# Layer norm of two graph layers: from ScalarE with relu to VectorE without, relu in the copy after the transpose

## The chip, the cores and the metric

The kernel runs on one core of a Trainium2 chip. The core has five engines that run side by side, each with its own queue of instructions in a fixed order: TensorE (PE, with its weight loads PEld), VectorE (DVE), ScalarE (ACT), GpSimd (POOL) and SyncE (SP). [...] The metric is the device time of one execution in microseconds (us), as the median of several runs; 0.2% of it is about 10 us.

## The reference

64 graphs of 256 nodes with 128 features each, and one 256 x 256 matrix `adj` for all. Four layers follow each other; each takes a layer norm without learned scale, a relu, and a graph layer, and adds the result:

```
h = maximum(layernorm(x), 0);  x = x + layer0(h)   # attention over all pairs of nodes
h = maximum(layernorm(x), 0);  x = x + layer1(h)   # elu(h Wi), sigmoid gates, two products
h = maximum(layernorm(x), 0);  x = x + layer2(h)   # tanh-limited attention
h = maximum(layernorm(x), 0);  x = x + layer3(h)   # five gated steps
layernorm(x) = (x - mean) / sqrt(var + 1e-5)       # over the 128 features
```

Layer 0 is the costly one. For each pair (i, j) of nodes it needs sum over e of a[e] * leaky_relu(s1[i, e] + s2[j, e]) with 256 values of e, so 64 x 256 x 256 x 256 elements pass an elementwise engine before TensorE sums them. Layers 1, 2 and 3 are small products.

## The kernel before, in words

The 64 graphs go in 34 groups: 1, 1, thirty times 2, 1, 1. A group's node features lie as `[128 nodes, G, 128 features]`, with G = 4 blocks of 128 nodes in a group of two graphs and G = 2 in a group of one.

Pair work of layer 0 (class `Pairs`). A tile is 128 x 256 elements. ScalarE (L620) makes a tile with relu and a bias column, GpSimd (L625) with min and max, VectorE (L608) makes four at a time as a "half". Four of the 128 x 512 slices that TensorE multiplies (L673) form a batch; there are two batches for each of 32 rows of a graph, one for each half of e. Where five batches or more are ready for TensorE as a row begins, the row is "merged": only the first half of e is made as a tile, VectorE adds the second to it in place (L642, "merge"), and TensorE has one batch less to multiply. VectorE's and ScalarE's operand s2 is held in PSUM (`s_dve`, `s_act`), GpSimd's in SBUF. The tiles `r` have 10 buffers.

Everything else is written as generators that yield the name of the engine of their next step: `head` and `senders` (layer 0 ahead of the pairs), `softmax0` (behind them), `first_rest` (layers 1 and 2, and the norm of layer 3) and `last_rest` (layer 3). They stand in four chains. The loop at the end of the kernel is a planner: it keeps a clock for each engine, books a cost for each instruction (the helpers `dve`, `act`, `pool` and `mm`, and the costs in `Model`), and at each turn issues what can start first by its clocks. A chain has a due time for each step, so that its steps spread over the pair work. The order of the instructions on each engine is thus fixed when the kernel is built, and follows from the booked costs. A changed cost changes which engine gets the next tile, and which rows are merged.

The norm is `ln_relu`. VectorE takes the statistics (L418, L421). GpSimd forms ve = var + eps (L426), minus = -mean (L427), rstd = ve to the power -0.5 (L429) and shift = minus * rstd (L431), all with G columns. ScalarE forms h = relu(rstd * x + shift), one 128 x 128 block an instruction (L437), with two operands that are columns of one value per node. The G blocks are issued two by two. `transpose_blocks` then transposes h on TensorE into PSUM, and ScalarE copies it to SBUF (L452) for the whole group. Layers 1 and 2 use h for nothing but this transpose. Layers 0 and 3 also use h itself.

In layers 1 and 2 together there are 256 blocks in 68 norms (34 groups, two layers).

Of the kernel before, what the change touches and what calls it, by code (L numbers as in the profile page):

```python
# [8 lines left out]
F32 = mybir.dt.float32  # L9
AF = mybir.ActivationFunctionType  # L10
ALU = mybir.AluOpType

P = 128
# [13 lines left out]
def flat(t):  # L27
    return t.rearrange("p a b -> p (a b)")


def sizes(xt):

    blocks = xt.shape[1]
    return blocks, blocks // 2, blocks * P
# [19 lines left out]
def kernel(ctx: ExitStack, tc: tile.TileContext, ins: dict, out: bass.AP):  # L54
# [8 lines left out]
    bp = ctx.enter_context(tc.tile_pool(name="act", bufs=1))  # L63
    sp = ctx.enter_context(tc.tile_pool(name="small", bufs=3))
# [11 lines left out]
    def psum_a(shape, name):  # L76
        return ps_a.tile(shape, F32, tag="ps_a", name=name)
# [8 lines left out]
    def dve(n, pointers=0, more=0):  # L86
        model.op("dve", 66 + n * 1.042 + 60 * pointers + more)
        return nc.vector

    def act(n, pointers=0, sbuf=0, table=0, more=0):  # L90
        model.op("act", 40 + n * 0.833 + 42 * sbuf + (0, 103, 196)[pointers] + 49 * table + more)
        return nc.scalar

    def pool(ns):
        model.op("pool", ns)
        return nc.gpsimd

    def mm(out, lhsT, rhs, **flags):


        n = 1
        for d in rhs.shape[1:]:
            n *= d
        model.op("pe", max(n, 64) * 1.676)
        for c in range(4):
            nc.tensor.matmul(  # L106
                out[bass.ts(c, 32), :], lhsT=lhsT[:, bass.ts(c, 32)], rhs=rhs, **flags
            )

    def tr(out, src):  # L110
        mm(out, lhsT=src, rhs=ident, start=True, stop=True)
# [294 lines left out]

    def ln_relu(space, xt, tag, ln, when=None):

        G = xt.shape[1]
        for g in range(G):
            if g % 2 == 0:
                yield "dve", when
            if g == 0:
                st = sp.tile([P, G, 6], F32, tag=tag + "_st", name="bst", bufs=2)
                mv = sp.tile([P, G, 2], F32, tag=tag + "_mv", name="bmv", bufs=2)
            dve(P).bn_stats(st[:, g, :], xt[:, g, :])  # L418
        yield "dve"
        for g in range(G):  # L420
            dve(6, more=15).bn_aggr(mv[:, g, :], st[:, g, :])  # L421
        yield "pool"

        ve = sp.tile([P, G], F32, tag=tag + "_ve", name="bve", bufs=2)
        minus = sp.tile([P, G], F32, tag=tag + "_mm", name="bmm", bufs=2)
        pool(277).tensor_scalar(ve, mv[:, :, 1], 1.0, LN_EPS, ALU.mult, ALU.add)  # L426
        pool(150).tensor_scalar(minus, mv[:, :, 0], -1.0, 0.0, ALU.mult, ALU.add)  # L427
        rstd = sp.tile([P, G], F32, tag=tag + "_rs", name="brs", bufs=2)
        pool(1085).tensor_tensor(rstd, ve, neg_half[:, 0:G], ALU.pow)  # L429
        shift = sp.tile([P, G], F32, tag=tag + "_sh", name="bsh", bufs=2)  # L430
        pool(302).tensor_tensor(shift, minus, rstd, ALU.mult)  # L431
        for g in range(G):
            if g % 2 == 0:
                yield "act"
            if g == 0:
                h = space.tile([P, G, P], F32, tag=ln, name=tag, bufs=3 if space is ap else 1)
            act(P, 2, 1).activation(  # L437
                h[:, g, :], xt[:, g, :], AF.Relu, bias=shift[:, g : g + 1],
                scale=rstd[:, g : g + 1],
            )  # L440
        return h

    def transpose_blocks(space, src, tag, banks):

        yield "pe"
        G, _, W = sizes(src)
        tp = banks([P, G, P], tag + "_ps")
        for g in range(G):
            tr(tp[:, g, :], src[:, g, :])
        yield "act"  # L450
        t = space.tile([P, G, P], F32, tag=tag, name=tag)
        act(W).copy(t, tp)  # L452
        return t


# [295 lines left out]

    def layer1(x1):
        G, NB, W = sizes(x1)
        h = yield from ln_relu(bp, x1, "h1", "h")
        h_t = yield from transpose_blocks(bp, h, "h_t", psum_a)
        yield "pe"
        xh_ps = psum_a([P, W], "xh_ps")
        mm(xh_ps, lhsT=wi, rhs=flat(h_t), start=True, stop=True)
        xh_t = yield from elu(xh_ps, bi, "xh_t", "xh_t")

        for b in range(NB):
            yield "pe"
            y_ps = psum_a([P, 2, P + 1], "y1_ps")
            for c in range(2):
                mm(
                    y_ps[:, c, :], lhsT=xh_t[:, bass.ts(2 * b + c, P)], rhs=wn1,
                    start=True, stop=True,
                )
            yield "act"
            if b == 0:  # L770
                y = bp.tile([P, G, P], F32, tag="y1", name="y1")
                a_src = sp.tile([P, G], F32, tag="a_src", name="a_src")
            act(N).copy(y[:, bass.ts(b, 2), :], y_ps[:, :, 0:P])
            yield "dve"
            dve(2, 1).tensor_scalar(
                a_src[:, bass.ts(b, 2)], y_ps[:, :, P], 0.5, be_h, ALU.mult, ALU.add
            )
        yield "pe"
        tgt_ps = psum_a([P, W], "tgt_ps")
        mm(tgt_ps, lhsT=wt_rep, rhs=xh_t, start=True, stop=True)  # L780
        yield "pool"
        x1b = bp.tile([P, G, P], F32, tag="x1b", name="x1b")
        counts["x1"] += 1
        pool(1265).tensor_tensor(
            x1b, x1, bm_bc.unsqueeze(1).to_broadcast([P, G, P]), ALU.add
        )

        ths, e_ts = [], []
        for b in range(NB):
            yield "act"  # L790
            th = bp.tile([P, 2, N], F32, tag="th", name="th", bufs=2)
            for jc in range(2):
                act(N, 1).activation(
                    th[:, jc, :], tgt_ps[:, bass.ts(b, N)], AF.Tanh,
                    bias=a_src[:, 2 * b + jc : 2 * b + jc + 1], scale=0.5,
                )
            ths.append(th)
        for b in range(NB):
            yield "dve"
            e_t = bp.tile([P, 2, N], F32, tag="e_t", name="e_t", bufs=2)  # L800
            dve(2 * N, more=200).scalar_tensor_tensor(e_t, ths[b], 1.0, mask_h, ALU.add, ALU.mult)
            e_ts.append(e_t)
        yield "pe"
        rsum_ps = psum_a([P, W], "rsum_ps")
        for b in range(NB):
            for jc in range(2):
                mm(
                    rsum_ps[:, bass.ts(b, N)], lhsT=ones, rhs=e_ts[b][:, jc, :],
                    start=(jc == 0), stop=(jc == 1),
                )  # L810
        yield "dve"
        self_t = bp.tile([P, W], F32, tag="elu_m", name="self_t")
        dve(W).tensor_tensor(self_t, rsum_ps, xh_t, ALU.mult)
        yield "pe"
        rc_ps = psum_a([P, W], "rc_ps")
        for b in range(NB):
            for jc in range(2):
                mm(
                    rc_ps[:, bass.ts(b, N)], lhsT=y[:, b * 2 + jc, :], rhs=e_ts[b][:, jc, :],
                    start=(b == 0 and jc == 0), stop=False, skip_group_check=True,  # L820
                )
        mm(rc_ps, lhsT=wn2, rhs=self_t, start=False, stop=True, skip_group_check=True)
        rc_t = yield from elu(rc_ps, bn, "rc_t", "h")
        yield "pe"
        o1_ps = psum_a([P, G, P], "o1_ps")
        for g in range(G):
            mm(
                o1_ps[:, g, :], lhsT=rc_t[:, bass.ts(g, P)], rhs=wm[:, 0, :], start=True, stop=False
            )
            mm(  # L830
                o1_ps[:, g, :], lhsT=xh_t[:, bass.ts(g, P)], rhs=wm[:, 1, :], start=False, stop=True
            )
        yield "dve"
        x2 = bp.tile([P, G, P], F32, tag="x2", name="x2")
        dve(W).tensor_tensor(x2, o1_ps, x1b, ALU.add)
        return x2

    def layer2(x2, when):
        G, NB, W = sizes(x2)
        h = yield from ln_relu(bp, x2, "h2", "h")  # L840
        h_t = yield from transpose_blocks(bp, h, "h_t", psum_a)
        yield "pe"
        g_ps = psum_a([P, W], "g_ps")
        mm(g_ps, lhsT=qk, rhs=flat(h_t), start=True, stop=True)
# [202 lines left out]
    while True:  # L1047
        paced = n < len(graphs) - 2
        if not making and n < len(graphs) and "s2" in sent[n]:
            g, b = graphs[n]  # L1050
# [96 lines left out]
```

## Time and profile before

| what | us |
|---|---|
| median of 3 runs | 5171.33 (5164.48 to 5172.37) |
| profiled execution | 5160.42 |
| its span | 5158.4 |
| TensorE busy | 5066.5 |
| ScalarE busy | 5032.3 |
| VectorE busy | 4983.9 |
| GpSimd busy | 4895.8 |

The profile is of one execution. It gives each instruction's start and end, the engine, the line of the kernel and the tiles it writes and reads. In a row of groups the columns are line, engine, operation, written tile <- read tiles, shapes and count, then the busy time in us and the mean duration of one in ns, and then the time that the engine stood idle just before such instructions, with what ended it. Rows of the stages give the stretch, its length, the busy time of the five engines with counts, the granted TensorE clock and the DMA share. A row of waits gives who waited for whom, the sum in us, how often, and the longest. A duration is not always what an instruction costs: on ScalarE several records overlap, so that the step from one instruction to the next is shorter than the duration of either.

### The profile page before, as it was taken

Reading aid. Unit: us, or ns where it says so; the run is one execution under the profiler, and the core shown is the slowest. Engines: PE = TensorE matmul, PEld = TensorE weight load, DVE = VectorE, ACT = ScalarE, POOL = GpSimd, SP = SyncE. Lnnn points to the kernel's source line nnn. Section 1 sums busy time; section 2 is a strip of 40 time slices with the busy share of each in tenths; the row PEclk is TensorE's granted clock in tenths of the full one; section 3 lists DMA queues with packets and bytes.
Section 4 is the critical chain, followed back from the end, with each engine's and each line's share of the span. In section 5 each row is a group of like instructions: output and inputs, shape, how many; then the busy total and the mean of one; then the engine's idle time right before and its main releaser. Section 6 shows DMA issues by size and latency. Waiting matters only on the chain. (4 is left out here: it accounts for less than half of the span.)

```text
span 5158.4 us, 172489 instructions
## 1 busy us (share of the span) xinstructions
PE 5066.5 (98%) x66800; PEld 2359.4 (46%) x66800; DVE 4983.9 (97%) x9900; ACT 5032.3 (98%) x13224; POOL 4895.8 (95%) x10829
## 2 busy tenths in 40 slices
PE   8999999999999999999999999999999999999996
PEld 4545444436444444544444544544444444444443
DVE  7999999999999999999999999999999999999993
ACT  7999999999999999999999999999999999999993
POOL 8999999999999999999999999999999999999991
PEclk9999999999999999999999999999999999999999
DMA  0000000000000000000000000000000000000000
GB/s 21 6 2 5 5 6 6 6 2 6 6 6 6 2 6 6 6 6 6 2 6 6 6 6 2 6 6 6 6 3 5 6 6 5 5 2 4 6 4 6
DMA packets 56104, 29.33 MB, mean 6 GB/s; under 512 B 20336, under 2 KB 55280, under 8 KB 55280
## 3 DMA queue, kind: packets, MB, share of 16 engines
q1 hardware_dynamic: 53168, 17.97, 1.4%
q8 instruction: 523, 8.57, 0.7%
q14 instruction: 301, 2.47, 0.2%
q10 hardware_dynamic: 2112, 0.33, 0.0%
HBM read 9.84 MB, written 8.45 MB: 4 GB/s over the span
## 5 line engine op out<-in xcount | busy, mean ns | idle before, releaser
L625 POOL TENSOR_SCALAR r<-s,s1n 128x256 f32<-128x256 f32 x10204 | 4646.6, 478 | 101.6 <-PE e_ps L673 33.9
L620 ACT ACTIVATE r<-s_act,s 128x256 f32<-128x256 f32 x9976 | 4593.3, 1478 | 10.5 <-PE e_ps L673 10.4
L673 PE MATMUL e_ps<-r,a_win 128*32 128x512 f32 x27632 | 3380.6, 593 | 8.3 <-DVE r L642 2.8
L642 DVE SCALAR_TENSOR_TENSOR r<-s_dve,s1n,r 128x256 f32<-128x256 f32 x5136 | 2094.4, 472 | 2.5 <-ACT r L620 1.5
L608 DVE TENSOR_TENSOR r<-s_dve,s1n 128x1024 f32<-128x1024 f32 x1735 | 2017.6, 1211 | 7.3 <-PE e_ps L673 1.4
L673 PEld LDWEIGHTS e_ps<-r,a_win 128*32 128x32 f32 x27632 | 1098.4, 110 | 1590.4 <-issue 1124.7
L620 ACT ACTIVATE r<-s,s 128x256 f32<-128x256 f32 x512 | 381.2, 1667 | 0.0
L437 ACT ACTIVATE h<-x,bsh,brs 128x128 f32<-128x128 f32 x384 | 329.5, 1384 | 3.6 <-POOL bsh L431 2.3
L929 ACT ACTIVATE gate_ps<-gate_ps,bz 128x512 f32<-128x512 f32 (+1 forms) x170 | 269.6, 1586 | 7.6 <-PE gate_ps L106 7.6
L910 ACT COPY m_t<-m_ps 128x512 f32<-128x512 f32 (+1 forms) x170 | 260.9, 1535 | 13.9 <-PE m_ps L106 13.9
L931 ACT ACTIVATE hv_ps<-hv_ps,bh 128x512 f32<-128x512 f32 (+1 forms) x170 | 266.4, 1567 | 7.6 <-PE hv_ps L106 7.6
L106 PE MATMUL m_ps<-adj_t,hn 128*32 128x256 f32 x4096 | 269.0, 381 | 3.7 <-ACT hn L452 3.6
L916 ACT ACTIVATE m_ps<-gate_ps,br 128x512 f32<-128x512 f32 (+1 forms) x170 | 256.8, 1511 | 10.9 <-PE gate_ps L106 10.7
L452 ACT COPY hn<-hn_ps 128x512 f32<-128x512 f32 (+1 forms) x136 | 208.1, 1530 | 24.1 <-PE hn_ps L106 24.0
L106 PEld LDWEIGHTS m_ps<-adj_t,hn 128*32 128x32 f32 x4096 | 157.4, 110 | 113.2 <-issue 32.3
L697 ACT ACTIVATE pm<-e_ps,nmax 128x256 f32<-128x256 f32 x128 | 194.5, 1526 | 2.2 <-DVE nmax L688 2.2
L106 PE MATMUL gate_ps<-m_t,t_w_w 128*32 128x512 f32 (+1 forms) x1360 | 187.9, 574 | 8.7 <-ACT m_t L910 7.7
L106 PE MATMUL gate_ps<-m_t,w_t 128*32 128x512 f32 (+1 forms) x1360 | 185.2, 568 | 4.9 <-ACT m_ps L916 4.9
L106 PE MATMUL hv_ps<-m_t,t_w_w 128*32 128x512 f32 (+1 forms) x1360 | 185.1, 568 | 0.0
L106 PE MATMUL hv_ps<-rh,u_th 128*32 128x512 f32 (+1 forms) x1360 | 184.9, 567 | 0.0
L106 PE MATMUL hn_ps<-ident,hf 128*32 128x128 f32 x4096 | 162.8, 274 | 19.8 <-DVE hf L941 19.8
L106 PEld LDWEIGHTS hn_ps<-ident,hf 128*32 128x32 f32 x4096 | 136.4, 110 | 84.5 <-issue 62.5
(206 smaller groups left out, 5952.2 us busy)
## 6 DMA issues: line engine op xcount, KB each, us to landing
xt<-in_x_dram SPq DMA_DIRECT2D x30, 256.0 KB
out_dram<-y SPq DMA_DIRECT2D x30, 256.0 KB
row<-rows SPq DMA_DIRECT2D x128, 0.5 KB
xt<-in_x_dram SPq DMA_DIRECT2D x4, 128.0 KB
out_dram<-y SPq DMA_DIRECT2D x4, 128.0 KB
bound<-row SPq DMA_DIRECT2D x30, 2.0 KB
raw_L_gnn_w_w<-in_L_gnn_w_w_dram SPq DMA_DIRECT2D x3, 128.0 KB
adj_n<-in_adj_dram ACTq DMA_DIRECT2D x1, 256.0 KB
```

The source lines that it names most:

```text
L106: nc.tensor.matmul(out[bass.ts(c, 32), :], lhsT=lhsT[:, bass.ts(c, 32)], rhs=rhs, **flags)
L437: act(P, 2, 1).activation(h[:, g, :], xt[:, g, :], AF.Relu, bias=shift[:, g : g + 1], scale=rstd[:, g : g + 1],)
L452: act(W).copy(t, tp)
L608: nc.vector.tensor_tensor(r[:, 2 * g2 : 2 * g2 + 2, :, :], s2[:, ec : ec + 1, :].unsqueeze(1).to_broadcast([P, 2, 2, N]), self.s1n_v[:, ec ...
L620: nc.scalar.activation(r[:, g, ic, :], s2[:, ec, :], AF.Relu, bias=s1[:, ec, i : i + 1])
L625: nc.gpsimd.tensor_scalar(r[:, g, ic, :], s2[:, ec, :], FLT_MAX, s1n[:, ec, i : i + 1], ALU.min, ALU.max,)
L642: nc.vector.scalar_tensor_tensor(r[:, g, ic, :], self.own("dve")[:, 1, :], self.of["s1n"][:, 1, i : i + 1], r[:, g, ic, :], ALU.max, ALU.add,)
L673: nc.tensor.matmul(self.e_ps[bass.ts(g, 32), :, :].rearrange("p a b -> p (a b)"), lhsT=a_win[:, batch["ec"], 31 - t : 63 - t], rhs=flat(r[ ...
L910: act(W).copy(m_t, m_ps)
L916: act(W, 1).activation(t_r, g_ps, AF.Tanh, bias=br, scale=0.5)
L929: act(W, 1).activation(t_z, g_ps, AF.Tanh, bias=bz, scale=0.5)
L931: act(W, 1).activation(cand, hv_ps, AF.Tanh, bias=bh)
```

## The change

For layers 1 and 2, `ln_relu` no longer forms minus and shift on GpSimd, and ScalarE no longer forms h. VectorE forms (x - mean) * rstd instead, block by block, from SBUF to SBUF, with the mean and rstd columns as operands. The relu, which now is missing there, is taken after the transpose: the copy from PSUM to SBUF becomes an activation with relu. Relu works element by element, so that its place before or after the transpose makes no difference to h. Layers 0 and 3 stay as they were. The planner books the new costs, and so plans the whole program anew.

```diff
-    def ln_relu(space, xt, tag, ln, when=None):
+    def ln_relu(space, xt, tag, ln, when=None, relu=True):
...
         ve = sp.tile([P, G], F32, tag=tag + "_ve", name="bve", bufs=2)
-        minus = sp.tile([P, G], F32, tag=tag + "_mm", name="bmm", bufs=2)
         pool(277).tensor_scalar(ve, mv[:, :, 1], 1.0, LN_EPS, ALU.mult, ALU.add)
-        pool(150).tensor_scalar(minus, mv[:, :, 0], -1.0, 0.0, ALU.mult, ALU.add)
+        if relu:
+            minus = sp.tile([P, G], F32, tag=tag + "_mm", name="bmm", bufs=2)
+            pool(151).tensor_scalar(minus, mv[:, :, 0], -1.0, 0.0, ALU.mult, ALU.add)
         rstd = sp.tile([P, G], F32, tag=tag + "_rs", name="brs", bufs=2)
         pool(1085).tensor_tensor(rstd, ve, neg_half[:, 0:G], ALU.pow)
-        shift = sp.tile([P, G], F32, tag=tag + "_sh", name="bsh", bufs=2)
-        pool(302).tensor_tensor(shift, minus, rstd, ALU.mult)
+        if relu:
+            shift = sp.tile([P, G], F32, tag=tag + "_sh", name="bsh", bufs=2)
+            pool(302).tensor_tensor(shift, minus, rstd, ALU.mult)
         for g in range(G):
             if g % 2 == 0:
-                yield "act"
+                yield "act" if relu else "dve"
             if g == 0:
                 h = space.tile([P, G, P], F32, tag=ln, name=tag, bufs=3 if space is ap else 1)
-            act(P, 2, 1).activation(
-                h[:, g, :], xt[:, g, :], AF.Relu, bias=shift[:, g : g + 1],
-                scale=rstd[:, g : g + 1],
-            )
+            if relu:
+                act(P, 2, 1).activation(
+                    h[:, g, :], xt[:, g, :], AF.Relu, bias=shift[:, g : g + 1],
+                    scale=rstd[:, g : g + 1],
+                )
+            else:
+                dve(P // 2, 1, more=20).tensor_scalar(
+                    h[:, g, :], xt[:, g, :], mv[:, g, 0:1], rstd[:, g : g + 1],
+                    ALU.subtract, ALU.mult,
+                )
         return h

-    def transpose_blocks(space, src, tag, banks):
+    def transpose_blocks(space, src, tag, banks, relu=False):
...
         t = space.tile([P, G, P], F32, tag=tag, name=tag)
-        act(W).copy(t, tp)
+        if relu:
+            act(W, table=1).activation(t, tp, AF.Relu)
+        else:
+            act(W).copy(t, tp)
         return t
...
     def layer1(x1):
-        h = yield from ln_relu(bp, x1, "h1", "h")
-        h_t = yield from transpose_blocks(bp, h, "h_t", psum_a)
+        h = yield from ln_relu(bp, x1, "h1", "h", relu=False)
+        h_t = yield from transpose_blocks(bp, h, "h_t", psum_a, relu=True)
...
     def layer2(x2, when):
-        h = yield from ln_relu(bp, x2, "h2", "h")
-        h_t = yield from transpose_blocks(bp, h, "h_t", psum_a)
+        h = yield from ln_relu(bp, x2, "h2", "h", relu=False)
+        h_t = yield from transpose_blocks(bp, h, "h_t", psum_a, relu=True)
```

## The prediction

> **What bounds the kernel now.** I read the page first: busy shares, the chain that ended last, the costliest groups.
>
> ```profile
> PE 5066.5 (98%) x66800; PEld 2359.4 (46%) x66800; DVE 4983.9 (97%) x9900; ACT 5032.3 (98%) x13224; POOL 4895.8 (95%) x10829
> ...
> PE 12%; ACT 9%; DVE 2%; issue 1%; POOL 0%; ACTq 0%; POOLq 0%; DVEq 0%
> ...
> L625 POOL TENSOR_SCALAR r<-s,s1n 128x256 f32<-128x256 f32 x10204 | 4646.6, 478 | 101.6 <-PE e_ps L673 33.9
> L620 ACT ACTIVATE r<-s_act,s 128x256 f32<-128x256 f32 x9976 | 4593.3, 1478 | 10.5 <-PE e_ps L673 10.4
> ...
> L642 DVE SCALAR_TENSOR_TENSOR r<-s_dve,s1n,r 128x256 f32<-128x256 f32 x5136 | 2094.4, 472 | 2.5 <-ACT r L620 1.5
> L608 DVE TENSOR_TENSOR r<-s_dve,s1n 128x1024 f32<-128x1024 f32 x1735 | 2017.6, 1211 | 7.3 <-PE e_ps L673 1.4
> ...
> L437 ACT ACTIVATE h<-x,bsh,brs 128x128 f32<-128x128 f32 x384 | 329.5, 1384 | 3.6 <-POOL bsh L431 2.3
> ```
>
> No engine is idle, so shares don't name the bound. Then the split by stage (start, pair phase, tail), and ScalarE's waits in the pair phase:
>
> ```profile
> 0.00:60.00 60.00, 44.76 (x480) 17.77 (x484) 33.05 (x89) 27.75 (x70) 39.17 (x97) 0.91 0.15 38
> 60.00:5039.00 4979.00, 4943.12 (x65012) 2304.46 (x65008) 4915.54 (x9728) 4966.61 (x13068) 4851.58 (x10718) 1.00 0.02 5
> 5039.00:5158.40 119.40, 78.57 (x1320) 37.16 (x1312) 35.27 (x85) 37.98 (x89) 5.08 (x16) 0.96 0.02 6
> ...
> ACT r L620 <- PE e_ps L673: 6.4, 7, 2.6
> ACT m_ps L916 <- PE gate_ps L106: 2.7, 3, 1.1
> ACT h L437 <- POOL bsh L431: 1.4, 3, 0.7
> ```
>
> The columns are PE, weight loads, DVE, ACT, POOL. In 4979 us ScalarE waits about 12 us in all. A record of ScalarE overlaps its neighbours (mean 1478 ns), so I take costs from the records as the step from one end to the next: ScalarE tile 364 ns (mean 366), norm block L437 381, copy of a 128x512 block 476, GpSimd tile 454, VectorE half (L608, four tiles) 1132, merge (L642) 392. Cost times count leaves of the 4979 us: ScalarE 16 us of waiting beside 31 us of spread, VectorE 79, GpSimd 138. TensorE at 858 ns for a batch of eight passes, 54 and 27 ns for narrower passes, is left with 134. ScalarE is the late engine. The planner books 357 ns for its tile where the trace has 364 to 366, so it runs behind its plan, while VectorE and GpSimd keep theirs and wait. The chain agrees: 9% ScalarE against 2% VectorE.
>
> [...] The one table load in the trace is the first; I expect no other.
>
> Evidence on the new operation[...], from the timeline (start, length of the row, count; the last row is GpSimd beside the row above it):
>
> ```profile
> 7.28 1.11 DVE L264 TENSOR_SCALAR perm<-places,place,a_abs 128x128 f32<-128x128 f32 x4
> ...
> 165.15 0.68 DVE L801 SCALAR_TENSOR_TENSOR e_t<-th,mask_h 128x512 f32<-128x512 f32 x1
> ...
> 74.31 1.57 DVE L392 TENSOR_TENSOR raw_L_gnn_w_w<-raw_L_gnn_w_w 128x128 f32<-128x128 f32 x1
> ...
> 1314.76 2.85 DVE L801 SCALAR_TENSOR_TENSOR e_t<-th,mask_h 128x512 f32<-128x512 f32 x1
> ...
> 1314.60 3.27 POOL L625 TENSOR_SCALAR r<-s,s1n 128x256 f32<-128x256 f32 x6
> ```
>
> L264 has the new form exactly (128x128, SBUF to SBUF, two column operands) with GpSimd idle: one takes 342 ns, so the step is (1110-342)/3 = 256 ns. L801 and L392 have two SBUF inputs with GpSimd busy. L801 takes 0.68 us free, but its 64 run from 673 to 2854 ns, median 733; the 2854 ns one let four GpSimd tiles pass and then cost the fifth some 530 ns. By where in the GpSimd tile they start: from 0 to about 100 ns none waits, from 110 to 330 they wait until about 335 or 450, later ones rarely.
>
> **The change part by part.** Counts are those of the built program.
>
> - ScalarE loses 256 norm blocks: 256 x 0.381 = -97.5 us. 68 copies become relu (+12 ns each, taking the 488 ns of L866, an activation without columns): +0.8. The planner hands it 200 more tiles: 200 x 0.366 = +73.2. Sum **-23.5 us**.
> - GpSimd loses 68 times minus (151 ns) and shift (304 ns; 298 for two columns): -30.9. 28 more tiles at 454: +12.7. Sum **-18.2**. [...]between 0 (L364 and L367, [...]cost the GpSimd tile beside them nothing) and 150 ns each (beside L392); I take 30, +8 us, hidden in its 138 us of waits. At 150 it is +38, still hidden.
> - TensorE has 3 batches fewer: **-2.6**. It is no bound.
> - VectorE gains 256 operations of cost c, loses 63 halves (-71.3), gains 24 merges (+9.4).
>
> What c is decides. The planner books 66 + 64 x 1.042 + 60 + 20 = 213 ns. Lower bound 256, L264's. [...]for a block at a random place in the GpSimd tile, about 80 ns, and 25 for an occasional lost turn (one L801 of 64, one L392 of 3). The blocks stand in pairs: the second asks 256 ns after the first was let in, inside the next GpSimd tile's hold after a first that waited, so it waits some 195, otherwise some 90; mean 140. So c = 256 + (105 + 140)/2 = **378 ns**; the upper end I keep is 600 (lost turns common). VectorE then has 4900 - 71.3 + 9.4 + 96.8 = **4935 us**; ScalarE 4932 - 23.5 + 31 spread = **4940**. The block also brings VectorE a new wait, for rstd from GpSimd. ScalarE's wait on GpSimd at L437 was 1.4 us in the pair phase, so I cost it at nothing; were the power late, merges and halves would stand behind the block on VectorE's queue, TensorE's next batch would wait for those, and r buffers would come free later. [...]
>
> Two engines now stand level where one stood at the top with 16 us of waits. I add 30 us, between ScalarE's 16 and VectorE's 79: 4935 + 30 = 4965, that is **-14 us** for the pair phase.
>
> The start has no block of these layers. In the tail layer 3 of the last groups sets the end: the norms of the last group lie beside it, so their saving is worth nothing. But in the built order the last pair batch is followed by one 256-wide m_ps product and one gate product less (5047.4 to 5050.0 in the trace before): **-2.5**. GpSimd is idle there[...].
>
> Sum -16 on the profiled 5160.4 us (span 5158.4): about 5145. The runs' median, 5171.3, is 11 us higher, so I shift by the same: 5171 - 16 = **5155 us**.
>
> **Rivals.**
>
> - *Little contention; ScalarE stays the bound.* If c is at most 339 (where 4838 + 256 c + 30 reaches 4979 - 23.5 = 4955.5), the pair phase falls by ScalarE's 23.5 us: with the tail -26, **5145**. For: L364 and L367 ran beside busy GpSimd tiles with next to no delay. [...] Against: the L801 rows.
> - *A draw.* c near 450: each block of a pair is let in once per GpSimd tile. VectorE 4953 + 30 = 4983, +4 - 2.5: **5173**.
> - *Slower[...].* The place is the block pairs; the price is a lost turn of 451 ns or more. From c = 443 the time is no better than before, from 483 it is over 0.2% slower; at 600 VectorE has 4992 + 30 = 5022, +43 - 2.5: **5212**. For: the 1.57 and 2.85 us rows, two of 67. Against: the median L801 waits only 60 ns[...].
> - That the change doesn't do what it says: the built program shows the moved instructions, and the other blocks keep their counts. No chance given.
>
> **How the numbers follow.** Forecast 48%, ScalarE-bound 20%, draw 12%, starvation 20%. A measurement tells some 0.2% (10 us) from no change. Of the forecast, 40 points are faster and 8 within it (c up to 420 or so). Faster 0.40 + 0.20 = 0.60; same 0.08 + 0.12 = 0.20; slower 0.20. Range 5140 to 5186: below the second case by the spread of the runs, up through the draw and the beginning of starvation, leaving out its worse half and the luckiest few. The likeliest case's own range is 5147 to 5165.
>
> **What would show it.** The block on VectorE: a step near 378 ns, minimum durations near 342, many 150 to 250 longer, a few over 1 us. ScalarE's waits in the pair phase up from 12 us; VectorE's down from 79; GpSimd tiles beside a block longer than 474 ns. Still one table load. Pair phase ending near 5025. I am wrong on c if the block's median is near 342 (second case) or its mean above 600 (fourth); wrong on the bound if VectorE still waits 80 us and the time hasn't moved.

## The result and the profile after

The changed kernel takes **5224.07 us** (median of 5 runs, 5216.57 to 5231.55). The kernel before takes 5172.37 beside it (5 runs, 5164.48 to 5175.45). The ratio is 1.0099, with an interval of 1.0087 to 1.011: about 52 us slower, where 16 us faster was forecast. The profiled execution took 5216.57 us, its span is 5214.7.

The page of the kernel after: busy times, the chain that ended last, and the costliest groups.

```profile
PE 5083.4 (97%) x66776; PEld 2396.5 (46%) x66776; DVE 5088.6 (98%) x10117; ACT 5024.6 (96%) x13168; POOL 4909.7 (94%) x10721
...
PE 1%; ACT 1%; DVE 1%; issue 0%; ACTq 0%; DVEq 0%
...
L637 POOL TENSOR_SCALAR r<-s,s1n 128x256 f32<-128x256 f32 x10232 | 4686.8, 522 | 131.9 <-PE e_ps L685 62.8
L632 ACT ACTIVATE r<-s_act,s 128x256 f32<-128x256 f32 x10176 | 4445.1, 1195 | 21.7 <-PE e_ps L685 21.1
...
L654 DVE SCALAR_TENSOR_TENSOR r<-s_dve,s1n,r 128x256 f32<-128x256 f32 x5160 | 2105.6, 469 | 0.6 <-POOL r L637 0.4
L620 DVE TENSOR_TENSOR r<-s_dve,s1n 128x1024 f32<-128x1024 f32 x1672 | 1944.0, 1208 | 7.1 <-PE tgt_ps L106 0.5
```

VectorE's busy time is up by 105 us, ScalarE's and GpSimd's hardly move. The counts are the planned ones. The chain is followed back only a short way here and tells nothing. By stage (stretch, then busy time of PE, weight loads, DVE, ACT, POOL):

```profile
0.00:60.00 60.00, 44.59 (x476) 17.66 (x480) 33.03 (x89) 27.67 (x70) 39.28 (x97) 0.91 0.15 38
60.00:5095.00 5035.00, 4959.96 (x65011) 2341.52 (x65004) 5014.17 (x9927) 4960.80 (x13017) 4866.61 (x10615) 1.00 0.02 5
5095.00:5214.70 119.70, 78.80 (x1304) 37.32 (x1296) 41.43 (x104) 36.10 (x83) 3.80 (x10) 0.95 0.02 6
```

The whole loss lies in the pair phase: the weights of the last pair product are loaded at 5105.3 us, before at 5046.6, and from there to the end it is 109.4 us against 111.8. In that phase ScalarE now waits for VectorE; in the kernel before its largest wait was 6.4 us:

```profile
ACT rc_ps L757 <- DVE elu_m L755: 22.4, 24, 2.1
ACT r L632 <- PE e_ps L685: 17.1, 16, 4.5
ACT pm L709 <- DVE nmax L700: 13.9, 14, 1.8
```

In the same phase VectorE's own longest wait in sum is 1.1 us; in the kernel before (second row) it was 9.4:

```profile
DVE elu_m L755 <- PE rc_ps L106: 1.1, 2, 0.6
...
DVE rc_t L749 <- ACT elu_m L746: 9.4, 14, 1.3
```

VectorE is the bound. What fills it beyond the plan is not the new blocks (L446). It is an instruction that the change doesn't touch, e_t in layer 1: L813 here, L801 before. These are the rows of groups after (busy us, then mean ns of one):

```profile
L813 DVE SCALAR_TENSOR_TENSOR e_t<-th,mask_h 128x512 f32<-128x512 f32 x64 | 133.4, 2084 | 0.0
...
L446 DVE TENSOR_SCALAR h<-x,bmv,brs 128x128 f32<-128x128 f32 x256 | 106.9, 457 | 2.6 <-POOL brs L431 2.5
```

and this is the same row of the kernel before:

```profile
L801 DVE SCALAR_TENSOR_TENSOR e_t<-th,mask_h 128x512 f32<-128x512 f32 x64 | 51.7, 808 | 0.0
```

Those 64 instructions cost VectorE 82 us more. The timeline after, at the longest of them (start, length, count; then who waited):

```profile
4817.00 9.66 POOL L637 TENSOR_SCALAR r<-s,s1n 128x256 f32<-128x256 f32 x20
4818.90 6.96 DVE L813 SCALAR_TENSOR_TENSOR e_t<-th,mask_h 128x512 f32<-128x512 f32 x1
...
4825.91 1.93 PE L106 MATMUL rsum_ps<-e_t,ones 128*32 128x256 f32 x16 [3.77 <-DVE e_t L813]
```

The e_t at 4827.31 us, with no GpSimd tile beside it, takes 0.68 us. The one at 4818.90 takes 6.3 us more, and fourteen GpSimd tiles start in its time, some 453 ns apart. Each tile that starts during such a wait is a lost turn below. VectorE starts nothing else until 4825.78, and TensorE waits 3.77 us. No list of waits has this wait, and e_t's idle time before it is 0.0. It shows only as a long record. 30 of the 64 take over 1.1 us; in the profile before it was one.

One more difference counts below. The mean record of a GpSimd tile is 522 ns here and was 478 before, although the step from tile to tile stays at 451 to 454 ns. Within a row of tiles without a pause the records grow by about 1.3 ns a tile, so that each comes to overlap the next by 100 to 150 ns in place of 20 to 30. I call such executions "growing" and the others "quiet". In the runs from here on a trace shows the first of several executions, and its kind need not be that of the others. In one run below, e12, the first took some 80 us less than the others, so that its ratio means nothing; I use medians there.

### The profile page after: what moved, and what is told of

Read it like the earlier page. It is cut to its first block, busy times and chain, and to the rows that moved or that the text cites. A ratio compares the mean times of both kernels' runs of the same rounds, so it can differ in the third digit from the quotient of the medians.

```text
span 5214.7 us, 172615 instructions
## 1 busy us (share of the span) xinstructions
PE 5083.4 (97%) x66776; PEld 2396.5 (46%) x66776; DVE 5088.6 (98%) x10117; ACT 5024.6 (96%) x13168; POOL 4909.7 (94%) x10721
## 5 line engine op out<-in xcount | busy, mean ns | idle before, releaser
L632 ACT ACTIVATE r<-s_act,s 128x256 f32<-128x256 f32 x10176 | 4445.1, 1195 | 21.7 <-PE e_ps L685 21.1
L685 PE MATMUL e_ps<-r,a_win 128*32 128x512 f32 x27608 | 3427.5, 593 | 18.3 <-DVE r L654 14.0
L620 DVE TENSOR_TENSOR r<-s_dve,s1n 128x1024 f32<-128x1024 f32 x1672 | 1944.0, 1208 | 7.1 <-PE tgt_ps L106 0.5
L922 ACT COPY m_t<-m_ps 128x512 f32<-128x512 f32 (+1 forms) x170 | 207.3, 1219 | 26.0 <-PE m_ps L106 26.0
L941 ACT ACTIVATE gate_ps<-gate_ps,bz 128x512 f32<-128x512 f32 (+1 forms) x170 | 220.6, 1298 | 6.8 <-PE gate_ps L106 6.6
L928 ACT ACTIVATE m_ps<-gate_ps,br 128x512 f32<-128x512 f32 (+1 forms) x170 | 210.9, 1241 | 16.0 <-PE gate_ps L106 12.3
L943 ACT ACTIVATE hv_ps<-hv_ps,bh 128x512 f32<-128x512 f32 (+1 forms) x170 | 219.1, 1289 | 7.3 <-PE hv_ps L106 7.3
L106 PE MATMUL gate_ps<-hf,u_t 128*32 128x512 f32 (+1 forms) x1088 | 164.7, 573 | 0.0
L106 PE MATMUL s_ps<-h0t,w_p 128*32 128x256 f32 (+1 forms) x1568 | 160.4, 449 | 4.1 <-ACT s1n L487 2.5
```

What stands on the lines that cost most here:

```text
L106: nc.tensor.matmul(out[bass.ts(c, 32), :], lhsT=lhsT[:, bass.ts(c, 32)], rhs=rhs, **flags)
L620: nc.vector.tensor_tensor(r[:, 2 * g2 : 2 * g2 + 2, :, :], s2[:, ec : ec + 1, :].unsqueeze(1).to_broadcast([P, 2, 2, N]), self.s1n_v[:, ec ...
L632: nc.scalar.activation(r[:, g, ic, :], s2[:, ec, :], AF.Relu, bias=s1[:, ec, i : i + 1])
L685: nc.tensor.matmul(self.e_ps[bass.ts(g, 32), :, :].rearrange("p a b -> p (a b)"), lhsT=a_win[:, batch["ec"], 31 - t : 63 - t], rhs=flat(r[ ...
L922: act(W).copy(m_t, m_ps)
L928: act(W, 1).activation(t_r, g_ps, AF.Tanh, bias=br, scale=0.5)
```

## The experiments

Theory 1: e_t's lost turns are the whole loss. Theory 2: the loss is the plan's (new order, the blocks as such), and the long e_t only shows it. Theories A, B and C then ask why e_t loses more turns after the change: A, the blocks of layer 1 ahead of it disturb GpSimd; B, the whole plan has shifted; C, GpSimd lacks the small operations minus and shift. (In the expectations of e1 and e2, A and B still stand for another question: whether the tiles grow by the program or by the chip.)

### Both kernels again (e1, e2), and e_t with an operand in PSUM (e3, e4)

e1 and e2 are the kernels as they are. e3 (before) and e4 (after) share this edit, here shortened. It leaves out the mask, so the values of e_t are others; the instruction, its size and its place stay:

```diff
-            dve(2 * N, more=200).scalar_tensor_tensor(e_t, ths[b], 1.0, mask_h, ALU.add, ALU.mult)
+            w = tgt_ps.rearrange("p (c n) -> p c n", n=N) if NB == 2 else ...   # the target product, in PSUM
+            dve(2 * N, more=200).scalar_tensor_tensor(e_t, ths[b], 1.0, w, ALU.add, ALU.mult)
```

> The kernel before, unchanged, profiled once more on the chip of the next runs. In the profile of the changed kernel GpSimd's tiles last 522 ns on the mean (478 before) because each ends a little later after its start than the one in front of it (about +1.3 ns a tile), and e_t lasts 2084 ns (808 before). Theory A, the changed program does this: here tiles stay near 474 to 478 ns and e_t near 0.8 us. Theory B, it is the chip or the day of the profile: here tiles creep too, and e_t exceeds 1.5 us.

> The changed kernel, unchanged, profiled on the same chip. Theory A: tiles near 520 ns, e_t near 2 us, time near 5224. Theory B: the same values as the kernel before has on this chip.

> The kernel before, with e_t = (th + 1) * (target product in PSUM) in place of the mask in SBUF: the mask is left out, the instruction, its size and its place are the same, but it has one SBUF input[...]. All theories: e_t falls from 0.81 to 0.68 us, 64 x 0.13 = 8 us of VectorE, which waits 79 us anyway: 5160 to 5172.

> The changed kernel with the same edit. Theory 1, the loss is e_t's lost turns[...] (64 x 1.28 us = 82 us more on VectorE): 5150 to 5165, that is 5 to 20 us under the kernel before with the same edit. Theory 2, the 256 blocks themselves overload VectorE (391 ns each) and the new order adds waits: the time stays 30 us or more over the kernel before with the same edit, 5200 or more.

On this chip before takes 5176.29 us (15 runs). e1 took 5174.08 and e2 5233.38, one execution each. The rows of e_t and of GpSimd's tile in e1:

```profile
L801 DVE SCALAR_TENSOR_TENSOR e_t<-th,mask_h 128x512 f32<-128x512 f32 x64 | 75.5, 1180 | 0.0
...
L625 POOL TENSOR_SCALAR r<-s,s1n 128x256 f32<-128x256 f32 x10204 | 4662.9, 530 | 100.4 <-PE e_ps L673 33.2 <-ACT s L514 16.5 <-ACT e_ps L726 13.0
```

and in e2:

```profile
L813 DVE SCALAR_TENSOR_TENSOR e_t<-th,mask_h 128x512 f32<-128x512 f32 x64 | 146.5, 2289 | 0.0
...
L637 POOL TENSOR_SCALAR r<-s,s1n 128x256 f32<-128x256 f32 x10232 | 4678.4, 526 | 152.9 <-PE e_ps L685 76.1 <-issue 29.7 <-ACT s L526 16.4
```

The kernel before can have growing tiles too (530 ns), so the change doesn't make them. With them its e_t takes 1.18 us in place of 0.81, between what the two theories gave, and 19 of 64 take over 1.1 us; the changed kernel's takes 2.29. With the operand in PSUM e_t takes 679 ns in e3 and, in e4:

```profile
L814 DVE SCALAR_TENSOR_TENSOR e_t<-th,tgt_ps 128x512 f32<-128x512 f32 x64 | 43.4, 678 | 0.4 <-ACT th L805 0.4
```

e3 stays where before is: 5172.67, ratio 0.9995 (0.9986 to 1.0004), though VectorE is rid of 32 us (64 x 0.5); the kernel before had room for them. e4 falls to **5155.81**, ratio 0.9961 (0.9946 to 0.9976): 78 us below e2, 17 below e3. Theory 1 holds, theory 2 falls. Between e3 and e4 stands the whole change, its blocks and its plan included, and it is worth those 17 us.

### One layer at a time (e5, e6)

e5 keeps the change in layer 1 only, e6 in layer 2 only; e5's edit:

```diff
     def layer2(x2, when):
-        h = yield from ln_relu(bp, x2, "h2", "h", relu=False)
-        h_t = yield from transpose_blocks(bp, h, "h_t", psum_a, relu=True)
+        h = yield from ln_relu(bp, x2, "h2", "h")
+        h_t = yield from transpose_blocks(bp, h, "h_t", psum_a)
```

> The change in layer 1 alone: 128 of the 256 norm blocks go to VectorE, those that stand between GpSimd's small operations of layer 1's norm and e_t of the same group; layer 2 keeps its norm on ScalarE. Results stay those of the reference. Theory A (the blocks disturb GpSimd between its last reset and e_t[...]): e_t as bad as with the whole change, mean near 2.2 us, and a time 55 to 70 us above before (half of the gain of 16, the whole loss). Theory B (e_t starves because the whole plan shifts: VectorE runs late, GpSimd and ScalarE run ahead): e_t half-way, mean 1.5 to 1.8 us, 20 to 40 us above before, the same for layer 2 alone.

> The change in layer 2 alone: the 128 blocks of layer 2 go to VectorE, those of layer 1 stay on ScalarE, so that between GpSimd's small operations of layer 1's norm and e_t no block of the same group stands on VectorE. Results stay those of the reference. Theory A: e_t as in the kernel before (mean near 1.0 to 1.2 us), and 5 to 10 us faster than before. Theory B: e_t mean 1.5 to 1.8 us, 20 to 40 us slower than before, as with layer 1 alone.

Before took 5178.92 us here. e5: **5237.86**, ratio 1.0123 (1.0106 to 1.014); e6: 5180.17, ratio 1.0004 (0.9998 to 1.0011). The row of e_t in e5:

```profile
L813 DVE SCALAR_TENSOR_TENSOR e_t<-th,mask_h 128x512 f32<-128x512 f32 x64 | 156.0, 2438 | 0.0
```

and in e6:

```profile
L813 DVE SCALAR_TENSOR_TENSOR e_t<-th,mask_h 128x512 f32<-128x512 f32 x64 | 95.0, 1485 | 0.1
```

Both had growing tiles (522 and 520 ns). Half of the change, put in layer 1, brings the whole loss; put in layer 2 it brings none, though no gain either, where 5 to 10 us were expected. Theory B, the same loss from both, falls. Theory A gets the times right; e6's e_t, at 1.49 us, is longer than it said (1.0 to 1.2) and than e1's 1.18 on another chip, so the blocks of layer 1 are perhaps not all that lengthens it.

### Versions with an operand of e_t in PSUM and with the mask (e7, e8)

The edit, condensed:

```diff
-        tgt_ps = psum_a([P, W], "tgt_ps")       # once; then th in SBUF for each graph, then e_t for each graph
+        for jc in range(2):
+            tgt_ps = psum_a([P, NB, N], "tgt_ps")
+            mm(flat(tgt_ps), lhsT=wt_rep, rhs=xh_t, start=True, stop=True)
+            for b in range(NB):
+                act(N, 1).activation(tgt_ps[:, b, :], tgt_ps[:, b, :], AF.Tanh, ...)
+            dve(W, more=200).scalar_tensor_tensor(
+                e_t, tgt_ps, 1.0, mask_h[:, jc : jc + 1, :].to_broadcast([P, NB, N]), ALU.add, ALU.mult)
```

> The kernel before, [...]the tanh is written in place over the target product in PSUM, for one half of the senders at a time, and TensorE makes the target product once more for the other half (34 to 38 more products of 512 columns, some 430 ns each, 15 us in all). e_t then has one operand in SBUF and one in PSUM. Expected: e_t near 680 ns, the time within 0.2% of before (e_t costs the kernel before 0.1 to 0.5 us each, and VectorE is not its bound). If the second product or the longer chain costs something on the path, up to 15 us slower.

> The changed kernel with the same edit, right results. If the loss is e_t's lost turns and nothing else: 14 to 20 us below before, thus some 70 below the changed kernel, faster than both. If TensorE's further products come on the path: up to 15 us less gain. If e_t's lost turns only move to another operation with two SBUF inputs: no better than before.

e7 (the kernel before with this edit): 5174.74, ratio 0.9995 (0.9986 to 1.0003). e8 (the changed kernel with it): **5167.31**, ratio 0.9978 (0.997 to 0.9986). e_t has a mean of 650 ns in both, and none takes over 693 ns. e8 is 12 us below before, a little less than the 14 to 20 expected. The changed kernel itself didn't run on this chip; with layer 1's half of the change (e5) it took 5237.86 here, 70 us more. Against e7 the change is worth 7 us here, not 17; where the other 10 go I didn't separate.

### The missing small operations of GpSimd (e9, e10, e13, e15)

Theory C lays the growth of e_t to minus and shift, which the change takes off GpSimd. e9 and e13 are one kernel: the changed one, with both formed and not used. e10 and e15 are one kernel too: the kernel before, with layer 1's minus and shift on ScalarE. Both edits are shortened.

```diff
-        if relu:
+        if True:
             minus = sp.tile([P, G], F32, tag=tag + "_mm", name="bmm", bufs=2)
```

```diff
-        pool(302).tensor_tensor(shift, minus, rstd, ALU.mult)
+        act(G, 1, sbuf=1).activation(minus, rstd, AF.Identity, scale=-1.0)
+        for g in range(G):
+            act(1, 1, sbuf=1).activation(shift[:, g : g + 1], minus[:, g : g + 1], AF.Identity, scale=mv[:, g, 0:1])
```

> The changed kernel with GpSimd's minus and shift kept in layers 1 and 2 (formed and not used; results stay right). The blocks stay on VectorE. GpSimd does 31 us more, of which it has some 50 to 140 us of waits. Theory C (the missing small operations after the power let GpSimd's tiles drift apart in another way): e_t mean back to 1.0 to 1.3 us and a time of some 5155 to 5180. Theory A (the blocks do it): e_t stays at 2.0 to 2.5 us and the time at 5225 to 5240.

> The kernel before, with minus and shift of layer 1 formed on ScalarE (five small instructions a group of two graphs) in place of GpSimd; the blocks stay on ScalarE, results stay right. ScalarE takes some 166 to 170 small instructions more, 30 to 40 us spread by the planner over three engines, so 10 to 20 us slower whatever e_t does. Theory C: e_t mean 2.0 to 2.5 us, and 60 us or more slower. Theory A: e_t mean 1.0 to 1.3 us.

e9: 5164.93 against 5164.06, ratio 1.0002 (0.9994 to 1.0011), e_t 1.11 us. e10: 5165.93, ratio 1.0005 (0.9996 to 1.0014), e_t 0.77. But on this chip all traces were quiet (477 and 481 ns), so e9's good time said nothing until the changed kernel itself had run beside it. Both were repeated on another chip with that control, e12:

> The changed kernel, unchanged, as the control for the next three on the same chip. In the last three runs no row of GpSimd tiles grew (tile mean 477 to 481 ns), as in the first profile of the kernel before, and unlike in the changed kernel's profile and in all runs before these three (519 to 533). If the chip decides how GpSimd's tiles lie: on one with quiet tiles the changed kernel takes 5150 to 5175 and e_t about 1.0 us; on one with growing tiles 5225 to 5240 and e_t over 2 us.

> The changed kernel with GpSimd's minus and shift kept and unused. Theory C (the missing small operations bring the loss): below the changed kernel by 40 us or more where tiles grow. Theory A (the blocks bring it): within 15 us of the changed kernel, either way.

> The kernel before with layer 1's minus and shift on ScalarE. Theory C: 40 us or more above before where tiles grow, e_t over 2 us. Theory A: within 15 us of before, e_t 1.0 to 1.3 us.

Before took 5177.09 us there. e13: **5243.08**, ratio 1.0121 (1.0105 to 1.0138). Its tiles and its e_t:

```profile
L637 POOL TENSOR_SCALAR r<-s,s1n 128x256 f32<-128x256 f32 x10200 | 4673.5, 518 | 145.3 <-PE e_ps L685 69.8 <-ACT s L526 16.6 <-issue 16.5
...
L813 DVE SCALAR_TENSOR_TENSOR e_t<-th,mask_h 128x512 f32<-128x512 f32 x64 | 153.6, 2400 | 0.1
```

e15: 5176.75, ratio 1.0 (0.9992 to 1.0009):

```profile
L636 POOL TENSOR_SCALAR r<-s,s1n 128x256 f32<-128x256 f32 x10240 | 4683.5, 521 | 84.5 <-PE e_ps L684 27.0 <-ACT s L525 16.6 <-issue 8.4
...
L812 DVE SCALAR_TENSOR_TENSOR e_t<-th,mask_h 128x512 f32<-128x512 f32 x64 | 59.2, 925 | 0.0
```

Both have growing tiles. Theory C falls from both sides: with the small operations kept the loss stays, and without them the kernel before loses nothing. Two expectations missed: e10 was to be 10 to 20 us slower for its added ScalarE instructions and is 2, and e15's e_t, at 0.92 us, is shorter than the 1.0 to 1.3 that theory A gave.

e12, the changed kernel as it is, falls in two. Its first execution took 5152.76 us and has this trace:

```profile
L637 POOL TENSOR_SCALAR r<-s,s1n 128x256 f32<-128x256 f32 x10232 | 4663.2, 477 | 90.5 <-PE e_ps L685 40.1 <-ACT s L526 16.5 <-issue 9.2
...
L813 DVE SCALAR_TENSOR_TENSOR e_t<-th,mask_h 128x512 f32<-128x512 f32 x64 | 64.2, 1003 | 0.0
```

Quiet tiles, then. The other 19, without a trace, took 5226 to 5240 (median of all 20: 5234.08). One program on one chip thus takes 5153 or some 5230 us. That the 19 had growing tiles, as e13 to e15 beside them, is likely but not shown. The kernel before took 5165.18 in its first execution there and then 5171 to 5183.

### A small GpSimd operation ahead of e_t (e11, e14, e16, e17, and the control e18)

The edit, with lines joined:

```diff
         for b in range(NB):
+            if b == 0:
+                yield "pool"
+                tick = sp.tile([P, 2], F32, tag="tick", name="tick", bufs=2)
+                pool(280).tensor_scalar(tick, ths[NB - 1][:, 1, N - 2 : N], 1.0, LN_EPS, ALU.mult, ALU.add)
             yield "dve"
             e_t = bp.tile([P, 2, N], F32, tag="e_t", name="e_t", bufs=2)
```

e11 and e14 are the changed kernel with it, e16 is the kernel before with it. In e17 (changed) it stands right behind layer 1's blocks instead, some 40 us earlier.

> The changed kernel with one small GpSimd operation (128 x 2, reads the last tanh of the group, its result is not used; results stay right) in GpSimd's queue ahead of the group's first e_t: a break in the row of tiles. If [...]such a break sets it back: overlap at e_t under 60 ns, e_t mean 0.7 to 1.0 us, and 5155 to 5165. If the overlap is only a mark of something else, or is not set back: e_t stays over 2 us and the time at 5225 to 5240.

> The changed kernel with one small GpSimd operation ahead of the group's first e_t. If [...]the small operation sets it back: 5150 to 5165 and e_t under 1.0 us on either kind of chip. Otherwise as the changed kernel, within 15 us.

> The kernel before with the same small GpSimd operation ahead of each group's first e_t. It saves VectorE some 20 us where e_t takes 1.18 us and nothing where it takes 0.8, and costs GpSimd some 10 us; VectorE is not this kernel's bound, as the run with e_t's operand in PSUM showed (0.9995). Expected: within 0.2% of before, e_t mean under 0.9 us.

> The changed kernel with the small GpSimd operation right behind layer 1's blocks (it reads the last block), some 40 us ahead of e_t, in place of right ahead of e_t. If the blocks leave GpSimd's row of tiles in a worse order that lasts until the next small operation: e_t as in the kernel before (0.8 us on quiet tiles, 1.0 to 1.3 on growing ones) and some 5160 to 5180. If what counts is the growth of the row up to e_t alone: e_t unchanged (over 2 us on growing tiles, about 1.0 on quiet ones), and the time as the changed kernel's.

> The changed kernel, unchanged, as the control on the same chip. On growing tiles 5225 to 5240 and e_t over 2 us; on quiet tiles 5150 to 5158 and e_t about 1.0 us.

e11: 5158.03 against 5164.06, ratio 0.9988 (0.9982 to 0.9995), but with quiet tiles and without the changed kernel beside it. e14: **5166.83** against 5177.09, ratio 0.9982 (0.9975 to 0.9989), on the chip on which the changed kernel had its median of 5234; the upper end expected was 5165. e14's rows:

```profile
L637 POOL TENSOR_SCALAR r<-s,s1n 128x256 f32<-128x256 f32 x10236 | 4685.0, 515 | 66.9 <-PE e_ps L685 17.2 <-ACT s L526 16.6 <-issue 6.3
...
L819 DVE SCALAR_TENSOR_TENSOR e_t<-th,mask_h 128x512 f32<-128x512 f32 x64 | 50.6, 790 | 0.0
```

The tiles grow (515), and yet e_t takes 0.79 us, the longest 1.07. The small operation stands a few tiles ahead of e_t (median 8), and in the pair phase no two tiles overlap by more than 38 ns while an e_t waits or runs; in the changed kernel's first trace it was up to 157 as an e_t began. So a break in GpSimd's row just ahead of e_t takes the loss away. The break is the operation together with a pause: GpSimd often stands idle before it until the tanh is there (median 0.4 us in e14). Which of the two does it was not separated.

e16: 5166.55 against 5173.28, ratio 0.9985 (0.9978 to 0.9992). I had expected no more than 0.2%, and that holds, but 7 us are gained where my reason (VectorE isn't the bound of the kernel before) left nothing to gain. What brings them isn't shown: an operand of e_t in PSUM brought that kernel 4 us in e3 and in e7, both within the noise. The kernel before with the small operation and the changed kernel with it stand alike against before, 0.9985 and 0.9982 to 0.9988; they were not run on one chip.

e17 asks where the break must stand. It and the two runs beside it had quiet tiles in their traces. On those e_t took 1.04 us in e17, nearer to 1.15 in the control e18 than to 0.81 in e16. On quiet tiles an early break thus helps little, against the theory that the blocks leave something behind which the next small operation clears; on growing ones it wasn't run. Its time, 5170.4 (ratio 0.9992), is no better than the control's.

The control is the surprise. e18, the changed kernel unchanged, took **5164.06** against 5173.28 there: ratio 0.9982 (0.9974 to 0.9991), *faster* than before. Its rows:

```profile
L637 POOL TENSOR_SCALAR r<-s,s1n 128x256 f32<-128x256 f32 x10232 | 4687.1, 480 | 81.5 <-PE e_ps L685 35.8 <-ACT s L526 16.7 <-issue 6.7
...
L813 DVE SCALAR_TENSOR_TENSOR e_t<-th,mask_h 128x512 f32<-128x512 f32 x64 | 73.5, 1148 | 0.0
```

This traced execution took 5171.66, though its tiles are quiet, and the other 13, without a trace, 5160 to 5168. On quiet tiles 5150 to 5158 had been expected; no part of the run reaches that.

## Why the prediction was wrong

**The cost of the new block was right.** Against the 378 ns of the prediction the 256 blocks take 391 on average from one end to the next: 361 for the first of a pair, as summed, and 421 for the second, where 396 was. The rival "Slower" needed c over 443 at the blocks. Its sign came true, but not at its place (the longest record of a block is 751 ns), so it would have been right by luck.

**The step that failed** is the one on the waits between VectorE and GpSimd: "between 0 ... and 150 ns each" for GpSimd's tile, and "for a block ..., about 80 ns, and 25 for an occasional lost turn", both estimates from the rows of L364, L367, L392 and L801. I costed the wait for the new instruction and for GpSimd, and used the rows of L801 as evidence for the blocks only. The time of L801 itself, which those rows show waiting beside GpSimd's tiles (up to 2.85 us), I left at its old 0.81 us; its growth stands at nothing in VectorE's 4935 us, and no reason is given. It went to 2.08: 64 x 1.28 = +82 us on VectorE, against the -16 of the sum. 82 - 16 = 66 is near the 59 us by which the pair phase grew; of the 30 us of waits in my sum VectorE has some 8 left. These 82 us mix a quiet trace with a growing one. On one chip, with growing tiles in both, e_t goes from 1.18 (e1) to 2.29 us (e2), and an operand in PSUM (e3, e4) is worth 4 us to the one kernel and 78 to the other.

**The second step that failed**: "The runs' median, 5171.3, is 11 us higher, so I shift by the same". The profiled execution had quiet tiles (478 ns). Later the kernel before took 5160 to 5172 (median 5164) on the chip of e9 to e11, where every trace was quiet, and 5172 to 5186 on those of e1 to e4 and e5 to e8, where every trace grew. The 11 us were probably the mark of executions of the other kind. That is argued: executions other than the profiled first one have no trace, and on the chip of e16 to e18 before took 5173 although the three traces were quiet. There the first execution of before took 5162 and the others 5170 to 5177. What e_t's waits cost isn't the same in the two kinds (a mean of 0.81 us in the first profile of before, 1.18 in e1), so a constant shift couldn't carry the sum over. My evidence on them, one long L801 of 64, was that of the kind in which e_t is seldom long; e1 has 19 of 64 over 1.1 us.

**The other steps.** The counts came as built. ScalarE's tile still steps by 365 ns (median) and the copy with relu by 488, as taken; there is one table load, as expected. The gain of 16 us appears in part where e_t is quick: 17 from e3 to e4, 7 from e7 to e8, 12 between the first execution of e12 and that of before on its chip, and 9 in e18. With the small operation in both kernels (e11 and e14 against e16, on different chips) nothing clear is left of it. The sum stands at the upper end of these; which of its terms is too large isn't shown. The tail was to save 2.5 us and saved 2.4. ScalarE's waits grew as said, above all those for VectorE. Two slips changed nothing: by its own terms the second case holds for c up to 341 ns, not 339, and the rows of L801 are less tidy than they were read: one that starts at 56 ns waits 0.28 us, and of the sixteen from 360 to 450 five wait 0.06 to 0.14.

**The rivals.** "ScalarE stays the bound" fails on c and on the waits. A draw is what e6 gave with half of the change, but for another reason. None named an old instruction as the one to starve.

**Who goes first.** In the 6.96 us above e_t stood first in VectorE's queue while fourteen tiles that came later went ahead: waiting longest brought no turn. What holds e_t up was not shown beyond this: with both operands in SBUF it waits beside GpSimd's tiles (a mean of 2.29 us in e2; 0.68 for each of the two that no tile ran beside in the changed kernel's first trace), and with one in PSUM it does not (0.68 in e4).

**What stays open.** Why layer 1's blocks, some 40 us ahead of e_t, make it lose more turns. It isn't a longer row of tiles: from GpSimd's last pause to the first e_t of a pair there are 90 tiles (median) in e2 and 89 in e1. It isn't minus and shift (e13, e15), and it isn't something that a small operation behind the blocks clears (e17, on quiet tiles). Overlap alone isn't it either. In the changed kernel's first trace all 24 of the e_t that met an overlap over 115 ns took over 1.1 us; in e15 only one of 25 did. On quiet tiles, with overlaps under 60 ns, the changed kernel still has 12 (e12) and 20 (e18) of 64 over 1.1 us. What makes tiles grow I don't know either. A block with its input in PSUM, to see whether its reading from SBUF does it, wasn't tried.

## What to carry to other kernels

Before you give VectorE an operation from SBUF to SBUF beside a GpSimd that never pauses, list the instructions with two SBUF inputs that already stand there and cost their waits anew; the new one may be cheap (391 ns here) and an old one starve (808 to 2084). Where a VectorE instruction with two SBUF inputs stands beside such a GpSimd, try one input in PSUM (2289 to 678 ns, e2 and e4) or a small GpSimd operation just ahead of it (790 in e14), and read its mean and its longest, not its median (733 before, 956 after, while the mean went from 808 to 2084). And if the profiled execution is 0.2% off the median of the runs, ask what differs between them before you carry a sum from one to the other.

## What the hardware showed beyond that

- GpSimd's tile records come in two kinds for the same program: about 478 ns, or growing by some 1.3 ns a tile to 600, at a step of 451 to 454 ns. The means are 478 and 530 for the kernel before (first profile, e1) and 522 and 477 for the changed one (first profile, e12).
- A VectorE instruction with two SBUF inputs lost up to fourteen turns in a row to GpSimd's tiles (6.96 us for 0.68 us of work), and with one input in PSUM took 693 ns at most (e7, e8). The second e_t of a pair, right behind such a one, took 0.99 us at most in the same trace.
- Whether the change loses or gains differs from chip to chip: 1.0099 in the first comparison, near 1.011 by medians in e12, but 0.9982 in e18. With e_t's long waits gone it gained each time, if little: 0.9961 (e4), 0.9978 (e8), and 0.9982 and 0.9988 (e14, e11).
